# Moving a branch ahead of a shared block, building a routing table block by block, and turning outputs later, in a four-layer kernel

## The chip, the core and the metric

The kernel runs on one core of a Trainium2 chip. The core has engines with queues of their own: TensorE (PE, matrix products and turns), VectorE (DVE), ScalarE (ACT), GpSimd (POOL), and SyncE (SP), which here only issues DMAs; ACT and POOL issue some too. Each engine works through its instructions in the order in which the program has them, and semaphores tie the engines together. The time is that of the device for one execution, in microseconds (us), as the median of several runs. The kernel before takes 2748.42 us (three runs, 2748.25 to 2751.44).

## What is computed

Four layers work on 2048 tokens (8 sequences of 256) of 512 channels. Each adds an attention-like part and a feed-forward part, every one behind a layer norm and scaled by a gate:

```python
x = x + tanh(g_xattn[l]) * xattn_l(layernorm(x), ctx)
x = x + tanh(g_ffn[l])   * ffn_l(layernorm(x))
```

Three of these parts matter here. Layer 1's feed-forward part chooses 8 of 64 experts for each token and adds a shared expert:

```python
out = moe_out + silu(x @ sh_gate) * (x @ sh_up) @ sh_down
```

Layer 2's part is gelu(x @ p1 + b1) @ p2 + b2 with 2048 hidden units. Layer 3's attention is a recurrence over the 256 tokens of a sequence, channel by channel (WKV, with running sums aa and bb and a running maximum pp); its feed-forward part takes the best 2 of 8 experts and a shared MLP:

```python
scores = softmax(x @ gate_w.T); topk_w, topk_i = top_k(scores, 2)
eo = (silu(x @ w_gate[e]) * (x @ w_up[e])) @ w_down[e]      # of each expert e
y  = sum of topk_w * eo over the two choices + silu(x @ sw_gate) * (x @ sw_up) @ sw_down
```

## The kernel before

The tokens stand in 16 tiles of 128 (`P`), in 4 blocks of 512 (`BLK`, `NB` = 4, `TB` = 4 tiles). The 512 channels are 4 chunks of 128 (`KC`). The residual x of all tokens stays in SBUF. Three functions run one after the other: `front()` is layer 0, `middle()` layer 1, `back()` layers 2 and 3. A scheduler places each engine's instructions by the order in which the program makes them and by what they depend on; `behind(one, other)` and `held` add hints of order without a wait. Pools of a fixed number of buffers decide when a buffer can be used again: `t2` has 8 tiles of 128x512, `mm`, `tr` and `ac` are PSUM.

**The end of layer 1.** Every routed pair of tiles (`Pair`, 56 of them) loads an expert's weights, gathers its tokens, and runs gate and up products, a turn on PE (`turn`), and down products (`down`, L1286), whose result POOL adds to a table in memory, `acc`, by an indirect accumulating DMA. `shared1(blk)` is the shared expert of a block: three products (shg, shu, shr), then two steps of down products (shd). For the last block it is made as `end`, and `experts1` takes the first three of its steps as `between`, ahead of the last pair's turn; the rest comes after the last pair. Only then come a read of a flag and a branch (L1328 to L1332) to further pairs of tiles, which run only if more experts need a second tile than were planned for; with these inputs they don't.

```python
end = shared1(NB - 1, again)
experts1(pairs, (next(end) for _ in range(3)))
for _ in end:
    pass
some = nc.values_load(needing[0:1, 0:1], ...)
with tc.If(some > PAIRS1):
```

**The start of layer 2.** `back()` first fills layer 3's empty table (`table`, 39 tiles of 128 rows of a token's number and a weight) and the zero rows of `xnd` on POOL, and SP writes them out. `combine` (L1343) loads what the experts added (`more<-acc`) and adds it to x; the norm and the first attention products of layer 2, s, follow.

**Layer 2 beside layer 3's recurrence.** `ffn2(blk)` runs 4 quarters of hidden units, each 4 times h2p (4 products of 0.86 us, each two records in the trace) and 4 times o2f (also 4 products). Beside it the generator `tail(blk - 1)` is advanced: `step(2)` after each h2p, `step(1)` after each o2f. A tail is `xattn3` (the recurrence, one pass of DVE, POOL and ACT for each of 4 chunks, then the turned result y is added to x, L1520) and `route` (norm f3, the router's logits, the best two). `held` places a step's DVE operation behind the add of the product of the other block. When the last quarter's first o2f is done, `step(1000)` runs what is left. For the last block, tail(3) is advanced by `shared3()`, the shared MLP: for each block six steps (m = 5, 0 to 4; products sg and su) and two of down products (sd). `step(2)`, five times `step(5)` and twice `step(3)` belong to a block. In `xattn3` the last block yields five times more ahead of y (L1514 and the line after).

**The routing of layer 3.** After `SH0` = 15 steps of `shared3` and what is left of the tail, the whole table is built at once: how many tokens chose each expert (`cnt`), each choice's place (`pos`, `key`), rows and weights (`row_i`, `pay`), and 32 indirect writes from POOL (L1878), one for each tile and choice. SP reads the table back (`slots`), after `SH1` = 7 more steps DVE casts the token numbers (`who`, L1899), and `routed(n)` runs for 36 tiles: POOL gathers the expert's weights w (L1903) and the tokens xg (L1912), PE turns xg (tr_xg), and the products follow, with the remaining 9 steps of `shared3` between them. The results of `shared3` (`ys`) are added to the output by DMAs that POOL issues (L1804).

Of the kernel before, what the change touches and what calls it, by code (L numbers as in the profile page):

```python
# [20 lines left out]
P = 128  # L21
C = 512
# [17 lines left out]
SH0, SH1 = 15, 7  # L40
# [6 lines left out]
def flamingo_kernel(ctx: ExitStack, tc: tile.TileContext, a):  # L47
# [83 lines left out]
    def behind(one, other, reason):  # L131

        tc.add_manual_dep(
            one.ins,
            other.ins.name,
            mybir.DependencyInfo(mybir.DependencyClass.NoSync, mybir.DependencyReason.SCHED_ONLY),
            reason=reason,
        )
# [504 lines left out]
    def middle():  # L643
        with ExitStack() as st:
# [592 lines left out]
            class Pair:  # L1237


                def __init__(self, c, alike):  # L1240
                    self.c, self.alike = c, alike
                    self.w = []
                    self.more = t2.tile([P, C], F32, tag="t2", name=f"wd{c}")
                    for n in range(1 if alike else 2):
                        e = nc.values_load(
                            order[0:1, c + n : c + n + 1],
                            engines=[mybir.EngineType.SP],
                            min_val=0,
                            max_val=E1 - 1,
                            skip_runtime_bounds_check_because="each of the 64 ranks is one expert's",  # L1250
                        )
                        one = bass.ds(e, 1)
                        self.w.append(weight(a["w1"][one].rearrange("o p c -> (o p) c"), f"w1_{c + n}", ahead=c < 4))
                        nc.sync.dma_start(
                            self.more[rows_of[n]], a["wd1"][one].rearrange("o p c -> (o p) c")
                        )
                    self.w = (self.w * 2)[0:2]
                    self.buf = b8.tile([P, 2, C + I1 + 2 * P], F32, tag="b8", name=f"eb{c}")
                    self.tiles = []
                    self.tile()  # L1260
# [33 lines left out]
            def experts1(pairs, between=()):  # L1294

                rest = None
                pair = Pair(*pairs[0])
                for n in range(len(pairs)):
                    act = pair.first(0)
                    if pair.alike:  # L1300
                        behind(nc.scalar.copy(pair.more[rows_of[1]], pair.more[rows_of[0]]), act, "it comes late")
                    pair.tile()
                    if rest is not None:
                        rest.tiles[1].turn()
                        rest.down()
                    rest = pair
                    if n + 1 < len(pairs):
                        pair = Pair(*pairs[n + 1])
                    rest.first(1)
                    rest.tiles[0].turn()  # L1310
                for _ in between:
                    pass
                rest.tiles[1].turn()
                rest.down()
# [9 lines left out]
            end = shared1(NB - 1, again)  # L1324
            experts1(pairs, (next(end) for _ in range(3)))
            for _ in end:
                pass
# [3 lines left out]
            with tc.If(some > PAIRS1):  # L1331
                experts1([(PAIRS1 + E1 + 2 * n, False) for n in range((E1 - PAIRS1) // 2)])  # L1332
# [80 lines left out]
    def ffn2(blk, b8, wp, b1, gb2, step, last):  # L1413
        xT = turned2.pop(blk)

        for q in range(HID // BLK):
            h = b8.tile([P, KC, BLK], F32, tag="b8", name=f"h2_{q}_{blk}")
            p2 = []
            for j in range(KC):
# [10 lines left out]
                step(2, one)  # L1430
# [17 lines left out]
    def xattn3(blk, b8, lp, u, w, held):  # L1448
# [65 lines left out]
        if blk == NB - 1:  # L1514
            yield from (None,) * 5
# [13 lines left out]
    def back():  # L1529
        with ExitStack() as st:  # L1530
# [13 lines left out]

            xnd = dp.tile([NT + P, C], F32, tag="xnd3", name="xnd3")
            table = dp.tile([P * NS3, 2], F32, tag="table3", name="table3")
            rows_of_slot = table.rearrange("(p n) c -> p n c", p=P)
            empty = lp.tile([P, NS3, 2], F32, tag="empty3", name="empty3")
            nc.gpsimd.memset(empty, 0.0)
            nc.gpsimd.iota(  # L1550
                empty[:, :, 0], pattern=[[0, NS3]], base=NT, channel_multiplier=1, allow_small_or_imprecise_dtypes=True
            )
            nc.sync.dma_start(rows_of_slot, empty)
            zero = t2.tile([P, C], F32, tag="t2", name="zero3")
            nc.gpsimd.memset(zero, 0.0)
            nc.sync.dma_start(xnd[NT : NT + P, :], zero)
# [15 lines left out]
            )  # L1572
            part = lp.tile([P, 1], F32, tag="part3", name="part3")
# [4 lines left out]
            nc.sync.dma_start(gw, a["gwT3"].rearrange("p (k e) -> p k e", k=KC))  # L1578
# [4 lines left out]
            nc.vector.memset(run[:, 0, :], 0.0)  # L1583
            xT = []

            def route(blk):
# [18 lines left out]
                for i in range(TB):  # L1605
                    t = blk * TB + i
                    nc.vector.tensor_tensor(run[:, t + 1, :], run[:, t, :], sel[:, t, :], ALU.add)

# [51 lines left out]
            first_loads.append(loaded)  # L1660
            loaded = combine(range(TB, 2 * TB))
# [156 lines left out]
            wide = [P, TT, 8]  # L1818
            cnt = ac.tile([P, 8], F32, tag="ac", name="cnt3")
            nc.tensor.matmul(cnt, onesb, run[:, TT, :], start=True, stop=True)  # L1820
            pos = ac.tile(wide, F32, tag="ac", name="pos3")
            nc.tensor.matmul(pos, before, sel, start=True, stop=False)
            nc.tensor.matmul(pos, onesb, run[:, 0:TT, :], start=False, stop=True)

            def tiles_of(dst, src, plus):

                nc.vector.tensor_scalar(dst, src, 1.0 / P, plus / P - 0.498, ALU.mult, ALU.add)
                nc.vector.tensor_scalar(dst, dst, ROUND, None, ALU.add)
                nc.vector.tensor_scalar(dst, dst, -ROUND, None, ALU.add)

            tl = lp.tile([P, 8], F32, tag="tl3", name="tl3")
            tiles_of(tl, cnt, P - 1.0)
            ends = lp.tile([P, 8], F32, tag="ends3", name="ends3")
            nc.vector.tensor_tensor_scan(
                out=ends, data0=tl, data1=zero[:, 0:8], initial=0.0, op0=ALU.add, op1=ALU.add
# [6 lines left out]
            base = lp.tile([P, 8], F32, tag="base3", name="base3")  # L1842
            nc.vector.scalar_tensor_tensor(base, ends, 1.0, tl, ALU.add, ALU.subtract)
            fl = lp.tile(wide, F32, tag="fl3", name="fl3")
            tiles_of(fl, pos, 0.0)
            key = lp.tile(wide, F32, tag="key3", name="key3")
            nc.vector.scalar_tensor_tensor(
                key, pos, float(NS3), base.unsqueeze(1).to_broadcast(wide), ALU.mult, ALU.add
            )
            nc.vector.scalar_tensor_tensor(key, fl, 1.0 - NS3 * P, key, ALU.mult, ALU.add)  # L1850
            nc.vector.tensor_tensor(key, key, sel, ALU.mult)
            first = lp.tile([P, TT], F32, tag="first3", name="first3")
            other = lp.tile([P, TT], F32, tag="other3", name="other3")
            nc.vector.tensor_reduce(first, key, AX.X, ALU.max)
            nc.vector.tensor_reduce(other, key, AX.X, ALU.add)
            nc.vector.tensor_tensor(other, other, first, ALU.subtract)
            row_i = lp.tile([P, TT, 2], I32, tag="row3", name="row3")
            for j, r in enumerate((first, other)):
                nc.vector.tensor_tensor(fl, key, r.unsqueeze(2).to_broadcast(wide), ALU.is_equal)
                nc.vector.tensor_tensor(fl, fl, comb, ALU.mult)  # L1860
                nc.vector.tensor_reduce(pay[:, :, j, 1], fl, AX.X, ALU.add)
                nc.vector.tensor_scalar(row_i[:, :, j], r, -1.0, None, ALU.add)
# [11 lines left out]

            writes = []
            for t in range(TT):
                for j in range(2):
                    one = nc.gpsimd.indirect_dma_start(  # L1878
                        out=table[:, :],
                        out_offset=bass.IndirectOffsetOnAxis(ap=row_i[:, t, j : j + 1], axis=0),  # L1880
                        in_=pay[:, t, j, :],
                        in_offset=None,
                    )
                    tc.declare_no_dep(one.ins, group="table3", reason="choices have slots of their own")
                    tc.add_to_no_dep_group("table3", one.ins)
                    writes.append(one)
            slots = lp.tile([P, NS3, 2], F32, tag="slots3", name="slots3")
            load = nc.sync.dma_start(slots, rows_of_slot)
# [7 lines left out]
            for n in range(SH1):  # L1896
                next(more)
            who = lp.tile([P, NS3], I32, tag="who3", name="who3")
            behind(nc.vector.tensor_copy(who, slots[:, :, 0]), last_mul[0], "the table comes late")  # L1899

            def routed(n, one_more=False):
# [31 lines left out]
                tile3(f"r{n}", xgT, wgu, slots[:, n, 1:2], wd, add)  # L1933
# [105 lines left out]
```

## Time and profile before

One execution was profiled. It took 2773.92 us, its span is 2772.2.

| stage (us of the span) | PE busy | DVE busy | POOL busy | PE clock granted |
|---|---|---|---|---|
| 1520 to 1552, end of layer 1 | 12.93 of 32 | 14.32 | 5.62 | 0.72 |
| 1552 to 2166, layer 2 and tails | 589.91 of 614 | 360.53 | 141.60 | 0.98 |
| 2166 to 2200, start of shared3 | 29.89 of 34 | 26.63 | 4.93 | 0.95 |
| 2200 to 2280, last recurrence | 75.03 of 80 | 54.23 | 33.45 | 0.98 |
| 2280 to 2391, routing | 88.15 of 111 | 29.97 | 46.83 | 0.91 |
| 2391 to 2772, routed tiles | 366.24 of 381 | 68.58 | 127.56 | 0.98 |

A line of the waits names the engine and what it would have run, what released it, and the microseconds in total, how often, and the longest. A line of the timeline has start, duration, engine, line, operation, output and inputs, and in brackets how long the engine had been idle and who released it. L174 is a line of the kernel as printed above. A product of 512 columns shows as two records; the granted clock is 1 at full rate.

### The profile page before, as it was taken

The page shows a single profiled execution, that of the slowest core. Times are in us where ns is not written, and L with a number is a line of the kernel's source. Part 1 is how long each engine was busy: PE and PEld are TensorE (multiplying, and loading weights), DVE is VectorE, ACT ScalarE, POOL GpSimd, SP SyncE. Part 2 cuts the span into 40 slices and gives each one's busy share as a digit, 9 for nine tenths or more (in the row PEclk, how much of TensorE's full clock was granted, in tenths as well). Part 3 has the DMA queues.
Part 4 walks back from the last instruction along what each step waited for, and adds up shares of the span by engine and source line. Part 5 has one row for each costly group of instructions (what it writes and reads, how often), then busy time and mean ns, then how long its engine had stood idle before and what let it go on. Part 6 is the DMA issues. An engine that isn't in the chain of part 4 may idle for free. (4 is left out here: it accounts for less than half of the span.)

```text
span 2772.2 us, 29438 instructions
## 1 busy us (share of the span) xinstructions
PE 2580.3 (93%) x10245; PEld 1364.2 (49%) x10260; DVE 1277.0 (46%) x3495; ACT 665.8 (24%) x1500; POOL 889.9 (32%) x812
## 2 busy tenths in 40 slices
PE   7889998999999899999999799899999989799998
PEld 3454544456555445555555244344444434355554
DVE  7657665446644622222222732768566763111111
ACT  2534343211111113333332111222222221011111
POOL 1111111113434445565554110322323243433332
PEclk9999999999999899999999899999999999899999
DMA  5000000111100159999996812021121212688985
GB/s 209 9 20 20 20 35 5 40 47 43 62 24 24 57 173 241 241 242 249 240 250 126 281 40 99 29 89 50 61 91 68 95 15 71 208 276 268 300 268 120
DMA packets 96281, 332.86 MB, mean 120 GB/s; under 512 B 20863, under 2 KB 23167, under 8 KB 88192
## 3 DMA queue, kind: packets, MB, share of 16 engines
q0 software_dynamic: 45808, 156.38, 22.6%
q1 hardware_dynamic: 47440, 170.30, 17.7%
q10 hardware_dynamic: 2880, 4.23, 0.5%
q8 instruction: 85, 1.39, 0.2%
q14 instruction: 68, 0.56, 0.1%
HBM read 280.37 MB, written 64.82 MB: 125 GB/s over the span
## 5 line engine op out<-in xcount | busy, mean ns | idle before, releaser
L207 PE MATMUL gu<-w,eb 128*128 128x352 f32 x896 | 285.7, 462 | 0.0
L1286 POOL DMA_INDIRECT acc<-eb,who x112 | 177.4, 1584 | 184.2 <-DVE eb L102 164.4
L207 PE MATMUL h2p<-xnT_f,p 128*128 128x512 f32 x512 | 228.3, 602 | 2.4 <-ACT xnT_f L104 2.4
L207 PE MATMUL o2f<-p,h 128*128 128x512 f32 x512 | 226.4, 597 | 0.7 <-ACT h L1429 0.7
L207 PEld LDWEIGHTS gu<-w,eb 128*128 128x128 f32 x896 | 162.6, 192 | 73.0 <-issue 2.3
L947 POOL DMA_INDIRECT table<-pay,rowi x128 | 126.1, 985 | 148.7 <-issue 27.2
L536 ACT ACTIVATE pr<-pr,n 128x256 f32<-128x256 f32 x256 | 127.9, 501 | 150.0 <-DVE n L531 147.1
L207 PEld LDWEIGHTS h2p<-xnT_f,p 128*128 128x128 f32 x512 | 98.0, 193 | 122.5 <-issue 117.6
L207 PEld LDWEIGHTS o2f<-p,h 128*128 128x128 f32 x512 | 96.9, 191 | 119.4 <-issue 115.6
L1206 POOL DMA_INDIRECT xg<-xnd,who x112 | 117.6, 1050 | 61.4 <-PE ehp L1233 23.1
L218 DVE SCALAR_TENSOR_TENSOR x<-o2f,tg,x 128x512 f32<-128x512 f32 x64 | 47.8, 749 | 160.8 <-PE o2f L207 160.8
L1696 PE MATMUL g_r<-w,xgT 128*128 128x352 f32 x288 | 111.9, 470 | 0.7 <-ACT xgT L104 0.7
L1429 ACT ACTIVATE h<-h2p,b 128x512 f32<-128x512 f32 x64 | 43.0, 686 | 288.9 <-PE h2p L207 288.8
L1696 PE MATMUL u_r<-w,xgT 128*128 128x352 f32 x288 | 108.7, 459 | 0.0
L188 PE MATMUL tr_xg<-ident,xg 128*128 128x128 f32 x592 | 93.3, 281 | 13.7 <-DMA xg<-xnd,who 13.7
L1277 PE MATMUL ed<-w,eb 128*128 128x512 f32 x224 | 105.4, 593 | 0.0
L1719 PE MATMUL d_r<-w,hT_r 128*128 128x512 f32 (+1 forms) x216 | 104.2, 592 | 0.0
L188 PEld LDWEIGHTS tr_xg<-ident,xg 128*128 128x128 f32 x592 | 69.0, 142 | 70.7 <-issue 50.6
L102 DVE COPY eb<-ed 128x512 f32<-128x512 f32 x56 | 38.7, 692 | 137.8 <-PE ed L1277 137.8
L531 DVE CUSTOM_DVE_ANT_0 pr<-s,mask 128x256 f32<-128x256 f32 x256 | 96.8, 416 | 11.6 <-PE s L511 8.2
L1703 DVE SCALAR_TENSOR_TENSOR h_r<-a_r,slots,u_r 128x352 f32<-128x352 f32 x36 | 20.9, 581 | 175.9 <-PE u_r L1696 172.7
L1223 DVE SCALAR_TENSOR_TENSOR eb<-eb,share,gu 128x176 f32<-128x176 f32 x112 | 44.0, 393 | 122.2 <-ACT eb L1222 77.7
(530 smaller groups left out, 4717.6 us busy)
## 6 DMA issues: line engine op xcount, KB each, us to landing
w<-in_w SPq DMA_DIRECT2D x64, 960.0 KB
p<-in_p SPq DMA_DIRECT2D x64, 512.0 KB
xnd<-xn_f SPq DMA_DIRECT2D x32, 256.0 KB
acc<-xnd SPq DMA_DIRECT2D x32, 256.0 KB
more<-acc SPq DMA_DIRECT2D x32, 256.0 KB
wd<-in_wd SPq DMA_DIRECT2D x64, 96.0 KB
ctxTa<-in_ctxT SPq DMA_DIRECT2D x4, 1024.0 KB
x<-in_x SPq DMA_DIRECT2D x16, 256.0 KB
```

Of the source, the lines that this page charges most:

```text
L188: one = nc.tensor.transpose(ps[:, k, :], src[:, ts(k, P)], ident)
L207: one = nc.tensor.matmul(ps, lhsT[k], rhs[k], start=(k == 0), stop=(k == n - 1))
L218: return nc.vector.scalar_tensor_tensor(xt[i], ps, scale, xt[i], ALU.mult, ALU.add)
L531: one = nc.vector.tensor_tensor_reduce(pr[:, nt, :], ps[r][:, nt, :], mask[:, nt, :], -1.0, -LOW, ALU.add, ALU.min, n16[:, nt, h : h + 1],)
L536: nc.scalar.activation(pr[:, nt, :], pr[:, nt, :], AF.Exp, bias=n16[:, nt, h : h + 1], scale=-1.0, accum_out=s16[:, nt, h : h + 1],)
L947: one = nc.gpsimd.indirect_dma_start(out=table[:, :], out_offset=bass.IndirectOffsetOnAxis(ap=rows, axis=0), in_=choice, in_offset=None, b ...
L1206: nc.gpsimd.indirect_dma_start(out=xg, out_offset=None, in_=xnd[:, :], in_offset=bass.IndirectOffsetOnAxis(ap=who[:, c : c + 1], axis=0), ...
L1223: nc.vector.scalar_tensor_tensor(self.h, self.h, share[:, c : c + 1], gu[:, I1 : 2 * I1], ALU.mult, ALU.mult)
L1277: one = nc.tensor.matmul(ps[n], t.hT[rows, k, :], wd, start=(k == 0), stop=(k == 1))
L1286: nc.gpsimd.indirect_dma_start(out=acc[n][:, :], out_offset=bass.IndirectOffsetOnAxis(ap=who[:, t.c : t.c + 1], axis=0), in_=t.x, in_offse ...
L1696: nc.tensor.matmul(ps[:, 0:I3], xTt[:, k, :], wgu[k][:, g, :], start=(k == 0), stop=(k == KC - 1))
L1719: one = nc.tensor.matmul(ps, hT[:cn, n, :], wd[n][:cn], start=(n == 0), stop=(n == 2))
```

## The change

Five things change.

- Layer 1: `experts1` no longer takes steps of the last shared block. The branch follows it at once, and `shared1(NB - 1)` runs as a whole after the branch. The branch's own pairs take buffers of `wpool`.
- Layer 3's table gets a region of 2048 rows for each expert. It is emptied after the first `combine` and `context(0)`, no longer at the start of `back()`. The router's weights gw are loaded by ACT, no longer by SP.
- `route(blk)` now computes places, rows and weights for its own block and issues the block's 8 writes. With the regions, a choice's row needs only its expert and its rank there, not the counts of all blocks.
- After the last block, only counts, tile numbers and the first row of each of the tiles are computed. POOL reads the table by one indirect gather of 128 rows of 1 KB, PE turns the two halves (tokens, weights), DVE and ACT copy them out.
- Steps: 3 instead of 2 after each h2p from the third quarter on; the last block yields 10 times, not 5, before y; SH0, SH1 are 18, 4 instead of 15, 7.

```diff
-SH0, SH1 = 15, 7
+SH0, SH1 = 18, 4
...
-            def experts1(pairs, between=()):
+            def experts1(pairs):
...
                     rest.first(1)
                     rest.tiles[0].turn()
-                for _ in between:
-                    pass
                 rest.tiles[1].turn()
                 rest.down()
...
-            end = shared1(NB - 1, again)
-            experts1(pairs, (next(end) for _ in range(3)))
-            for _ in end:
-                pass
+            experts1(pairs)
             some = nc.values_load(
...
             with tc.If(some > PAIRS1):
-                experts1([(PAIRS1 + E1 + 2 * n, False) for n in range((E1 - PAIRS1) // 2)])
+                experts1([(PAIRS1 + E1 + 2 * n, False, (wpool, "w")) for n in range((E1 - PAIRS1) // 2)])
+            for _ in shared1(NB - 1, again):
+                pass
...
-                step(2, one)
+                step(2 if q < 2 else 3, one)
...
         if blk == NB - 1:
-            yield from (None,) * 5
+            yield from (None,) * 10
...
-            table = dp.tile([P * NS3, 2], F32, tag="table3", name="table3")
+            table = dp.tile([(E3 * TT + 1) * P, 2], F32, tag="table3", name="table3")
+            halves = table.rearrange("(h p) c -> h (p c)", p=P)
...
-            nc.sync.dma_start(gw, a["gwT3"].rearrange("p (k e) -> p k e", k=KC))
+            nc.scalar.dma_start(gw, a["gwT3"].rearrange("p (k e) -> p k e", k=KC))
...
+                pos = ac.tile(wide, F32, tag="ac", name=f"pos3_{blk}")
+                one, other = nc.tensor.matmul(pos, before, sel[:, tb, :], start=True, stop=False), latest[0]
+                behind(one, other, "the choices take their time")
+                nc.tensor.matmul(pos, onesb, run[:, tb, :], start=False, stop=True)
+                key = lp.tile(wide, F32, tag="key3", name=f"key3_{blk}")
+                nc.vector.tensor_tensor(key, pos, e2048.unsqueeze(1).to_broadcast(wide), ALU.add)
+                nc.vector.tensor_tensor(key, key, best, ALU.mult)
...
+                for t in range(blk * TB, blk * TB + TB):
+                    for j in range(2):
+                        one = nc.gpsimd.indirect_dma_start(
+                            out=table[:, :],
+                            out_offset=bass.IndirectOffsetOnAxis(ap=row_i[:, t, j : j + 1], axis=0),
+                            in_=pay[:, t, j, :],
+                            in_offset=None,
+                        )
...
             context(0, loaded)
             first_loads.append(loaded)
+            emptied()
...
-            load = nc.sync.dma_start(slots, rows_of_slot)
+            load = nc.gpsimd.indirect_dma_start(
+                out=slots.rearrange("h p c -> h (p c)"),
+                out_offset=None,
+                in_=halves,
+                in_offset=bass.IndirectOffsetOnAxis(ap=row_t[:, 0:1], axis=0),
+            )
...
+            who_ps = tr.tile([P, 2, P], F32, tag="tr", name="who3_ps")
+            other = latest[0]
+            for n in range(2):
+                one = nc.tensor.transpose(who_ps[:, n, :], slots[:, :, n], ident)
+                if n == 0:
+                    behind(one, other, "the table comes late")
             who = lp.tile([P, NS3], I32, tag="who3", name="who3")
-            behind(nc.vector.tensor_copy(who, slots[:, :, 0]), last_mul[0], "the table comes late")
+            behind(nc.vector.tensor_copy(who, who_ps[:, 0, 0:NS3]), last_mul[0], "the table comes late")
+            share = lp.tile([P, NS3], F32, tag="share3", name="share3")
+            nc.scalar.copy(share, who_ps[:, 1, 0:NS3])
```

## The prediction

> **What bounds it now.** The page's first part says TensorE: 2580.3 of 2772.2 us busy, 93%, and no other engine over 46%. The chain of waits ends in one output DMA and says nothing here, so I read next what PE waits for (us in total, times, longest), since only idle or half-clock PE time can be won. The largest wait of the run, and those between 2140 and 2460:
>
> ```profile
> PE s L207 <- DVE xn_a__0_12289 L174: 19.1, 1, 19.1
> ```
>
> ```profile
> PE y L1520 <- POOL xnT_a L1510: 8.8, 2, 6.5
> PE tr_xg L188 <- DMA xg<-xnd,who: 8.3, 1, 8.3
> PE sd L1792 <- issue: 6.9, 4, 2.5
> PE tr_f L188 <- DVE xn_f L174: 4.2, 2, 3.8
> ```
>
> The first is the seam between layers 1 and 2; the others surround layer 3's routing. Elsewhere on the changed paths PE waits little. So the sum has three places. All durations are of the profiled execution (2773.92 us, 1.7 around its span). It lies 25.5 us, 0.9%, above the median of 2748.42; I carry differences over unscaled, since 0.9% of 25 us is 0.2.
>
> **Seam of layers 1 and 2.** From the timeline (start, us, engine and operation, [idle before <- releaser]):
>
> ```profile
> 1528.18 1.55 POOL L1286 DMA_INDIRECT acc<-eb,who  x1 [0.30 <-issue]
> 1535.77 0.17 POOL L1549 MEMSET empty<- 128x78 f32 x1 [6.04 <-DMA acc<-eb,who]
> 1542.63 1.43 DVE L1343 TENSOR_TENSOR x<-x,more 128x512 f32<-128x512 f32 x2 [3.88 <-DMA more<-acc]
> 1550.34 2.05 PE L207 MATMUL s<-xn_a__0_12289,kxvs 128*128 128x512 f32 x2 [19.07 <-DVE xn_a__0_12289 L174]
> ```
>
> An accumulate lands 7.6 us after its issue; the reads of acc, the norm and PE follow in series. Now block 3's shared products lie before it, half inside the last pair, half after. Moved behind the branch, they run while the accumulates land. The last pair's turn then follows at once (DVE's h reaches PE at about 1512.7, 0.7 us idle), and its down products end at about 1516.1. The first accumulate must wait for the previous one on the same table (issued at 1510.25 in the timeline, + 7.6 = 1517.9), the second issues near 1519.7 and lands near 1527.3, not 1535.8. PE meanwhile has shg, shu, shr (four products of 0.86 each, 3 x 3.43) and shd (14 records of 0.43, 6.02), to 1533.4. SP's loads of acc start about 1528.2, after shr, land at 1532.5; DVE's first add stands behind the four shared adds, which end at 1534.9; from add to s takes 7.7 us (1542.63 to 1550.34). So s starts at 1542.6: **7.7 us won**, 9.2 still idle. ACT has 2 us to spare: shg's silu stands behind the small loads that ACT issues (gw is now one of them) and behind an Exp that waits for the decay's landing, ends near 1525.4, and PE needs its product at 1527.4. The emptying of the new table and its three SP DMAs leave the head of this chain; the POOL memsets (about 1 us) now stand ahead of later norms, under the adds. The branch cost DVE 0.27 us here; later code behind it is not shown, so 0.3 to 3. Bounds: 3 to 10 won.
>
> **Blocks 0 and 1: the earlier y.** With step(3) for q>=2, tail(0) and tail(1) reach their y products in the third quarter's o2f, after 8 of its 16, instead of 6 products into the fourth quarter: 14 x 0.86 = 12 us earlier in PE's order. The chain behind y must keep up. Its last pass in tail(1) before, and the one in tail(2), which already runs without waits on o2f:
>
> ```profile
> 2007.66 0.75 DVE L218 SCALAR_TENSOR_TENSOR x<-o2f,tg,x 128x512 f32<-128x512 f32 x1 [2.08 <-PE o2f L207]
> 2011.10 0.75 DVE L218 SCALAR_TENSOR_TENSOR x<-o2f,tg,x 128x512 f32<-128x512 f32 x1 [1.29 <-PE o2f L207]
> 2014.53 0.75 DVE L218 SCALAR_TENSOR_TENSOR x<-o2f,tg,x 128x512 f32<-128x512 f32 x1 [2.08 <-PE o2f L207]
> 2015.20 3.34 DVE L1508 RECIPROCAL den<-den 128x512 f32<-128x512 f32 x1
> 2019.94 0.66 PE L1520 MATMUL y<-ident,xnT_a 128*128 128x128 f32 x4 [0.30 <-POOL xnT_a L1510]
> ...
> 2140.30 3.34 DVE L1508 RECIPROCAL den<-den 128x512 f32<-128x512 f32 x1
> ...
> 2161.24 3.35 DVE L1508 RECIPROCAL den<-den 128x512 f32<-128x512 f32 x1 [1.38 <-POOL bb L1464]
> 2166.01 1.09 PE L1520 MATMUL y<-ident,xnT_a 128*128 128x128 f32 x8 [2.38 <-POOL xnT_a L1510]
> ```
>
> DVE's idle 2.08 and 1.29 are evacuations ahead of the chain in DVE's order. With them a pass takes 27.5 us from reciprocal to reciprocal (1987.73, the one before this, to 2015.20); without, 20.9 (2140.30 to 2161.24). The changed order has both bb scans ahead of aa, which saves the 1.38 and one scan more: 18.3. Reciprocal at 1987.7 + 18.3 + 3.34 + POOL's 1.3 puts xnT_a at 2010.8; PE arrives at 1986.9 + 24 x 0.86 = 2007.5. So PE waits about 3.5 us, 3.2 more than now, and the same in tail(0).
>
> Here a rule speaks against the change. The Trainium skill ("TensorE: Matmul & The Clock Gate", HAM oscillation) says that PE gaps above about 3.4 us put it at half clock, and its table gives about 3.4 us of work to recover: 1.7 lost. The rows agree at both sides. After 6.47 us the granted clock of 2286 to 2292 was 0.52, that of the next 8 us 1.00, and sg took 5.79 instead of 3.60. After 3.80 tr_f took 1.54 instead of 1.09; after 2.38 y ran at full rate, 1.09 for 8. A gap of 3.5 lies on the edge: by the rule 1.7 a block, by the 2.38 row nothing; I take 1.0. **8.4 us lost** in two blocks; bounds 1 (chain in time) and 20.
>
> Each block also gets its eight table writes on POOL, 8 x 1.28 = 10.2 us (0.97 and 0.30 between them). Behind them in POOL's order stands rstd_a. From pos to tr_a PE has 18 us (block 0) and 16.6 (block 1); the key operations take some 3 us, then the writes end at +13.3, before rstd_a's input at +15: covered. Cover gone, each us is one of PE. pos itself is two small matmuls and some 15 DVE operations of 0.15 to 0.3 in DVE's idle time.
>
> **Layer 3's routing.** Block 2's y now finds the chain ready to 1.4 us and tr_f lies inside the last o2f. Waits of 2.38 and 3.80 go. But what is late next is shgu, layer 3's shared weights, four loads of 704 KB into buffers that the last o2f frees: issued at 2171.4, and sg began at 2176.55, so the landing lay beside these waits. Now it is bare, some 4 us, and y waits 1.4: with half the cold products saved only **1.6 us won** (-2 to 5).
>
> For the last block, y stands one step (sg and su, 6.87 us) later: PE, which was there at 2279.9, comes at 2279.9 - 1.6 + 6.87 = 2285.2, and the chain, 1.6 earlier too, ends at 2284.8. With the hand-over, 6.47 becomes about 0.5 and y starts at 2285.7. Then the table:
>
> ```profile
> 2366.27 0.97 POOL L1878 DMA_INDIRECT table<-pay,row  x1 [0.30 <-issue]
> 2367.23 1.95 POOL L1804 DMA_DIRECT2D out_dram<-ys  x2
> ...
> 2378.15 0.95 POOL L1912 DMA_INDIRECT xg<-xnd,who  x1 [5.07 <-issue]
> ```
>
> 32 writes ran from 2326.4 to 2367.2. They held the output DMAs behind them in POOL's order, these held t2 buffers, and so DVE and sd: the 6.9 of "issue". Then who and xg, which landed 12.4 us after its issue behind w of 2.2 MB each. Changed, only eight writes remain, some 2327.5 to 2337.8; w_0, the gather, w_1 to w_3 issue by 2345. PE's work from y to tr_xg, at full rate, is 82.3 us of the timeline's products (SH0 + SH1 is still 22, so none is added), less the one now ahead of y: from 2285.7, 6.87 taken off what follows, it arrives at about 2361. slots (128 KB, behind w_0) is there at 2348; PE's two transposes stand behind four products and come at 2352, then the copy of who, and xg issues at 2354. PE's small turns cost it 0.3. The Trainium skill ("DMA: Bandwidth & Descriptors", Anatomy of one DMA) prices 256 KB at 2.0 us + bytes/436 GB/s, 2.6: xg at 2357, no wait. The row speaks of a queue: w_1 issued at 2369.5 and xg landed 21 us later with it. From 2341.5 that is 2363, and four w are now in flight at once, where w_0 was long there before: 2365. I take the row. Of 22.9 us idle (y 6.5, two small waits 1.2, sd 6.9, xg 8.3) and 5.4 at half clock (sg 2.2, the last ten sd records 7.20 instead of 4.3, and 0.3) some 4.5 remain: **23.8 won**. Bounds 14 (xg at 2375) and 28. The routed loop after it keeps its order and its PE bound.
>
> **Sum:** -7.7 + 8.4 - 1.6 - 23.8 = -24.7; 2748.4 becomes **2724**.
>
> **Rivals.**
> 1. The routed table is not early: the gather waits for the write landings and xg for 8.9 MB of w. Xg at 2375 leaves 10 us more idle: 2734. For it: the 12.4 us above. Against: 30 us fewer writes ahead.
> 2. The y stalls stay small, the seam loses its cold restart too: 8 + 2 less, 2714. For: the 20.9 row is itself a contended pass. Against: 3.80 already went cold.
> 3. Slower: the chain behind y is bound by DVE, POOL and ACT, not by o2f. Four passes in a row take 27.5 us. If that stays, y waits 12.4 us in blocks 0 and 1, 12.1 more than now, and in block 2 (chain ready at 2140.3 + 27.5 + 4.6 = 2172.4, PE there at 2155.8) 16.6, 14.2 more; each with 2 us at half clock: 44 lost. Against it 31.5 won at seam and table: +13, 2761. It decides from passes of some 26.5 us, where three times 8 us more eat the 24.7. For it speaks that no other pass is shown at 20.9; against it, the idle rows above.
> 4. The change doesn't do what it says at the branch: code behind it comes late, or the accumulates still end the chain; the seam gains nothing: 2732.
>
> **Chances.** Forecast 0.48, with 2717 to 2731 its own; rival 1 0.17, rival 2 0.17, rival 3 0.10, rival 4 0.08. The range for 8 in 10, 2710 to 2740, takes in rivals 1, 2 and 4. A measurement of this kernel tells 0.2%, 5.5 us. Faster 0.87: all but rival 3 and a tail of rivals 1 and 4; within 0.05; slower 0.08, most of rival 3.
>
> **What would show it.** s after the seam at some 9 us of wait, with shd just before. y in blocks 0 and 1 at some 3.5 us each. No wait on sd "issue"; tr_xg at 3 to 8. sg at stage start behind shgu. Wrong if y waits 10 us, or rstd_a is released by table writes, or tr_xg still waits 8 or more.

## The result and the profile after

| | median us | runs | lowest to highest |
|---|---|---|---|
| before | 2748.49 | 8 | 2744.56 to 2752.11 |
| after | 2739.19 | 8 | 2735.15 to 2745.19 |

The ratio is 0.9966 (95% interval 0.9953 to 0.9979): 9.3 us faster (5.8 to 12.9), where 24.7 were forecast. The direction is right, and of the sum a good third is there.

The profiled execution of after took 2745.19 us, 6 above its median; its page begins so:

```profile
span 2743.4 us, 29494 instructions
...
PE 2570.1 (94%) x10253; PEld 1360.1 (50%) x10268; DVE 1283.8 (47%) x3535; ACT 671.7 (24%) x1505; POOL 894.0 (33%) x814
```

One thing spoils a look at absolute times: the first 1000 us of the program, which no kernel here changes, took 1011.2 us in the profile of before and 985.8 in that of after, and the kernel before had medians of 2748, 2767 and 2776 in the sets of runs that follow. So I compare times within one set, and profiles from layer 1's first product `gu` on. From it the two kernels end after 1761.0 and 1757.6 us. A single profile still tells no more than a few us: before and experiment 2, the same up to there, reach layer 2's first h2p 1.6 us apart.

What TensorE waits for, in the stretch from layer 2's start to the first routed tiles (1560 to 2450; us in total, times, longest), and, from the whole run, the seam:

```profile
PE y L1517 <- POOL xnT_a L1507: 12.0, 3, 4.5
...
PE tr_xg L188 <- DMA xg<-xnd,who: 4.3, 1, 4.3
PE tr_a L188 <- DVE xn_a L174: 4.2, 2, 3.9
PE sd L1839 <- DVE ys L1848: 4.2, 1, 4.2
```

```profile
PE s L207 <- DVE xn_a__0_12285 L174: 8.8, 1, 8.8
```

The big waits went as forecast: s from 19.1 to 8.8, tr_xg from 8.3 to 4.3, no y of 6.5 for the last block, no sd on "issue". What is new is y: 12.0 in three waits, where the blocks 0 to 2 had 0.3, 0.3 and 2.4. But the waits don't add up to the time, so each place has to be looked at.

**The seam.** TensorE's timeline, after:

```profile
1489.79 1.13 PE L1277 MATMUL ed<-wd,eb 48*128 48x512 f32 x4
1494.34 5.37 PE L207 MATMUL shg<-xnT_f,shgu 128*128 128x512 f32 x8 [3.42 <-DVE run L1590]
1499.55 3.60 PE L207 MATMUL shu<-xnT_f,shgu 128*128 128x512 f32 x8
1502.98 3.60 PE L207 MATMUL shr<-xnT_f,shgu 128*112 128x512 f32 x8
1506.41 5.91 PE L1117 MATMUL shd<-shd,shT 128*128 128x512 f32 x16
1521.18 2.08 PE L207 MATMUL s<-xn_a__0_12285,kxvs 128*128 128x512 f32 x2 [8.85 <-DVE xn_a__0_12285 L174]
```

Between the last expert product and shg nothing runs for 3.42 us, and shg then takes 5.37 instead of the 3.60 of its equal shu: half clock (the granted clock was 0.67 in shg's stretch, 1.00 in shu's). The releaser named, `run`, is DVE's first instruction behind the branch, and it was itself released by TensorE's sequencer (PEq):

```profile
1494.21 0.06 DVE L1590 MEMSET run<- 128x4 uint32 x1 [2.56 <-PEq L1326]
```

So the engines meet behind the branch, and TensorE came last. The records of the branch's line on the engines' sequencers show why (engine, operation, times; ns; start), first after, then before:

```profile
L1326 PEldq COMPARE_BRANCH  x1: 3892/3892/3892, 1490.1 to 1490.1; - x1
L1326 ACTq COMPARE_BRANCH  x1: 45/45/45, 1491.5 to 1491.5; - x1
L1326 DVEq COMPARE_BRANCH  x1: 76/76/76, 1491.6 to 1491.6; - x1
```

```profile
L1331 PEldq COMPARE_BRANCH  x1: 3727/3727/3727, 1525.9 to 1525.9; - x1
```

On TensorE the branch takes 3.9 us (and reading the flag ahead of it 1.1), on the other engines 0.05 to 0.08. Before, TensorE's sequencer took it 5.4 us ahead of the last shared product's end, beside products that were already queued. After, only 0.8 us of products are left when it takes it.

**y in blocks 0 and 1.** TensorE's timeline, after:

```profile
1824.63 1.12 PE L1517 MATMUL y<-ident,xnT_a 128*128 128x128 f32 x4 [4.47 <-POOL xnT_a L1507]
1825.54 5.35 PE L207 MATMUL o2f<-p,h 128*128 128x512 f32 x8
1830.73 0.60 PE L1517 MATMUL y<-ident,xnT_a 128*128 128x128 f32 x4
1831.16 3.60 PE L207 MATMUL o2f<-p,h 128*128 128x512 f32 x8
...
1994.95 1.12 PE L1517 MATMUL y<-ident,xnT_a 128*128 128x128 f32 x4 [4.47 <-POOL xnT_a L1507]
1995.86 5.53 PE L207 MATMUL o2f<-p,h 128*128 128x512 f32 x8
```

Both blocks wait 4.47 us, and the first y and eight records of o2f after it cost 2.3 and 2.5 us more than the next ones (granted clock 0.63 and 0.62).

**The routing.** POOL's timeline, after:

```profile
2332.57 0.97 POOL L1643 DMA_INDIRECT table<-pay,row  x1 [0.31 <-DMA table<-pay,row]
2333.85 1.02 POOL L1932 DMA_INDIRECT w<-in_w,wrow  x1 [0.30 <-DMA table<-pay,row]
2338.23 0.97 POOL L1904 DMA_INDIRECT slots<-table,row_t  x1 [3.37 <-DMA table<-pay,row]
...
2349.89 0.96 POOL L1941 DMA_INDIRECT xg<-xnd,who  x1 [6.92 <-DVE who L1926]
```

Eight writes instead of 32, the gather behind the last one's landing, and xg at 2349.9, which TensorE has at 2361.8: 11.9 us behind the w of 2.2 MB, as in the row that the forecast took (12.4). From the last block's first y to the first routed product (g_r) the new routing takes 80.9 to 81.5 us in the six profiles that have it with ten yields, the old one 107.2 to 108.7 in six. Of the difference 6.87 us are the step that now stands ahead of y.

### The profile page after: what moved, and what is told of

It is laid out like the page before. It is cut to its first block, busy times and chain, and to the rows that moved or that the text cites. A ratio compares the mean times of both kernels' runs of the same rounds, so it can differ in the third digit from the quotient of the medians.

```text
span 2743.4 us, 29494 instructions
## 1 busy us (share of the span) xinstructions
PE 2570.1 (94%) x10253; PEld 1360.1 (50%) x10268; DVE 1283.8 (47%) x3535; ACT 671.7 (24%) x1505; POOL 894.0 (33%) x814
## 3 DMA queue, kind: packets, MB, share of 16 engines
q1 hardware_dynamic: 47154, 170.34, 18.3%
## 5 line engine op out<-in xcount | busy, mean ns | idle before, releaser
L207 PE MATMUL h2p<-xnT_f,p 128*128 128x512 f32 x512 | 235.6, 617 | 2.6 <-ACT xnT_f L104 2.6
L1743 PE MATMUL u_r<-w,xgT 128*128 128x352 f32 x288 | 108.7, 459 | 0.0
L1750 DVE SCALAR_TENSOR_TENSOR h_r<-a_r,share,u_r 128x352 f32<-128x352 f32 x36 | 20.9, 580 | 176.1 <-PE u_r L1743 172.9
```

The source lines that it names most:

```text
L207: one = nc.tensor.matmul(ps, lhsT[k], rhs[k], start=(k == 0), stop=(k == n - 1))
L1743: nc.tensor.matmul(ps[:, 0:I3], xTt[:, k, :], wgu[k][:, g, :], start=(k == 0), stop=(k == KC - 1))
```

## The experiments

Three questions: what ate the seam's gain, what y's early place costs, and whether the rest is as large as the sum had it. Ratios are to the kernel before in the same set of runs.

**1. After, without layer 1's branch.** The path for more experts than planned is left out.

```diff
             experts1(pairs)
-            some = nc.values_load(...)
-            with tc.If(some > PAIRS1):
-                experts1([(PAIRS1 + E1 + 2 * n, False, (wpool, "w")) ...])
             for _ in shared1(NB - 1, again):
```

> The changed kernel without the branch of layer 1 (the read of its flag and the pairs of tiles behind it, which these inputs don't run; the path for overflowing experts is left out). Theory BRANCH: in the changed kernel PE's own compare-and-branch (3.9 us) and flag read (1.1) stand bare ahead of shg, and 3.4 us of idle time put shg at half clock (5.37 instead of 3.60). Without it shg follows the last down products at once: PE's wait before shg under 0.6, and 4 to 6 us less than the changed kernel (ratio to before near 0.995, from 0.9966). Rival ACCUMULATES: the seam is set by the landing of the last accumulates and the loads behind it; then shg comes early but s starts no earlier, its wait grows from 8.8 to about 13, and the time stays at 0.9966.

2736.57 us, ratio 0.9952 (0.9939 to 0.9966): 2.6 us under after by the medians, less than expected, and the two intervals overlap. The profile is plainer: no wait ahead of shg, and s 7.3 us earlier (528.0 us after gu, not 535.3), with its own wait unchanged:

```profile
1511.90 2.08 PE L207 MATMUL s<-xn_a__0_11733,kxvs 128*128 128x512 f32 x2 [8.86 <-DVE xn_a__0_11733 L174]
```

So s follows the shared products; the accumulates don't set it.

**2. Before, with step(3) alone.**

```diff
-                step(2, one)
+                step(2 if q < 2 else 3, one)
```

> The kernel before with one edit: step(3) instead of step(2) after h2p from the third quarter on. Theory Y-EARLY: y of tail(0) and tail(1) comes ahead of the end of its chain, PE waits 4.5 us there twice and runs at half clock after it; 10 to 14 us slower than before (ratio 1.004 to 1.005). Rival WRITES: what blocks 0 and 1 lose in the changed kernel comes from the eight table writes on POOL; then this kernel, which has none there, is within 0.1% of before. Rival CLOCK: the loss is half-clock stretches that come and go by themselves; then also within 0.1%.

2768.28 us, ratio 1.0072 (1.0058 to 1.0086): 19.9 slower, more than expected. TensorE's waits from 1560 to 2480:

```profile
PE tr_xg L188 <- DMA xg<-xnd,who: 20.7, 1, 20.7
PE y L1520 <- POOL xnT_a L1510: 18.4, 4, 6.5
```

No block has its table writes here, and y waits all the same: the writes are not its cause. From the first h2p of block 1 to that of block 2 it takes 170.3 us, before 163.1: 7.2 for one early y. The 20.7 at tr_xg is not the step's doing: experiment 4, which has the old steps, shows 20.1 there and no wait on sd "issue", and from the last y to the first routed product the two take 108.5 and 107.8 us, before 107.2. Two blocks at 7.2 make 14.4; the rest of the 19.9 is not explained, so it is not the price of y alone. Experiment 3 gives that.

**3. After, with y two steps later in blocks 0 to 2.**

```diff
-        if blk == NB - 1:
-            yield from (None,) * 10
+        yield from (None,) * (10 if blk == NB - 1 else 2)
```

> The changed kernel with two more yields ahead of y for the blocks other than the last, so that y of tail(0) and tail(1) stands 8 products (6.9 us) later on PE, while the steps stay quick. Theory Y-EARLY: the waits of 4.5 before y vanish in both blocks, with the half-clock products after them, and nothing else moves: 10 to 14 us less than the changed kernel (ratio to before 0.9915 to 0.993). Rival WRITES: the table writes are then nearer to rstd_a, and tr_a waits instead: no gain, 0.9966. Rival CLOCK: no gain either, and no wait before tr_a.

2726.57 us, ratio 0.9919 (0.9905 to 0.9932): 12.9 us less than after by the ratios (0.9966 - 0.9919 = 0.0047 of 2748), which by their intervals is an estimate of 8 to 18. The waits of blocks 0 and 1 are gone:

```profile
PE y L1516 <- POOL xnT_a L1507: 3.0, 1, 3.0
```

The rows above say the same: 4.47 - 0.3 in each of two blocks, and 2.3 and 2.5 at half clock, are 13.1. So this is the price of y's early place, and the chain needs only two steps. The two profiles lie further apart, 20.6 us from `gu` on. Some 3.6 of the rest is mostly half clock at the end of block 2, from the first y there to the first sg (27.8 us after, 24.2 in experiment 3); it is in the profiles of after and of experiment 1, and what sets it off is not known.

**4. Before, with the seam's part alone.**

```diff
-            end = shared1(NB - 1, again)
-            experts1(pairs, (next(end) for _ in range(3)))
-            for _ in end:
-                pass
+            experts1(pairs)
             some = nc.values_load(...)
             with tc.If(some > PAIRS1):
-                experts1([(PAIRS1 + E1 + 2 * n, False) ...])
+                experts1([(PAIRS1 + E1 + 2 * n, False, (wpool, "w")) ...])
+            for _ in shared1(NB - 1, again):
+                pass
```

> The kernel before with the first part of the change alone: the branch ahead of the whole last shared block. Theory BRANCH: 2 to 6 us faster than before (0.998 to 0.9993), with PE idle about 3.4 us before shg and some 9 to 12 before s, since the old emptying of the table still stands at the head of back() here. The prediction's own figure for this part was 7.7. Rival ACCUMULATES: the landing sets s and the seam gains the full 7 to 8 us (0.9972).

2748.62 us, ratio 0.9997 (0.9989 to 1.0005): nothing, where a gain was expected.

**5 and 6. Y later, with another seam.** In 5 shg, shu and shr stand ahead of the branch, behind the last pair, in a buffer of their own; in 6 the seam is that of before. All else is experiment 3.

```diff
             experts1(pairs)
+            end = shared1(NB - 1, again)
+            for _ in range(3):
+                next(end)
             some = nc.values_load(...)
...
-            for _ in shared1(NB - 1, again):
+            for _ in end:
                 pass
```

> The kernel with y later (changed kernel, two more yields), and shg, shu and shr of the last shared block made ahead of the branch, after the last pair, with buffers of b8 so that the branch's pairs don't wait for them; only shd stays behind the branch. Theory BRANCH: PE's sequencer stands at the branch while the matmuls already issued still run, as in the kernel before (its compare-and-branch of 3.7 us began 5.4 us ahead of the last shd's end), so the 3.9 us lie beside products: PE's wait at the branch under 1 us, 3 to 6 us less than y later alone (ratio to before 0.9897 to 0.9908). Rival FETCH: PE can't fetch behind a branch before it has drained; then some 3 us of wait stand ahead of shd and the time stays at 0.9919.

> The kernel with y later, its seam as in the kernel before (three shared products inside the last pair, the rest ahead of the branch). Theory BRANCH and the run of the seam alone: the branch's move is worth nothing where its 5 us stand bare; the time stays within 3 us of y later (0.991 to 0.993). Rival: the seam alone gained nothing only because the old emptying of the table stood at the head of back(); with it moved the new seam is worth 4 to 8, and this kernel is that much slower (0.9935 to 0.995).

Number 5: 2744.24 us beside 2776.27 of before in its set, ratio 0.9895 (0.9880 to 0.9910), the best of all kernels here, though its interval touches that of experiment 3. The hiding worked only in part: shd waits 2.05 us, not under 1, and then takes 9.23 us instead of the 5.91 of after. TensorE's own branch was covered. It ended at 1518.8, 2.7 us ahead of the end of shr; but the engines meet behind it, and here DVE came last, whose flag read and branch stand behind its product with shr:

```profile
L1334 PEldq COMPARE_BRANCH  x1: 4478/4478/4478, 1514.3 to 1514.3; - x1
L1334 DVEq COMPARE_BRANCH  x1: 76/76/76, 1522.8 to 1522.8; - x1
```

Number 6, in the same set: 2752.16, ratio 0.9917 (0.9904 to 0.9931), which is that of experiment 3 (0.9919). Once more the seam as changed is worth nothing. And number 6 holds all else of the change without the early y: 0.0083 of 2748, 22.8 us won.

**7 and 8. Other steps.** In 7, after with `step(2, one)` throughout; in 8, experiment 3 with 5 yields for the last block, not 10.

> The changed kernel with step(2) in all quarters, so that y stands where it stood before and the tails run as slowly as before. Theory Y-EARLY with a second term: the waits before y go (12 us), but pos of block 1 then comes only 8 us of PE's work ahead of tr_a, while the eight writes (10.2 us) and rstd_a stand between on POOL; tr_a of tail(2) waits 5 to 8 us and goes cold. Net 2 to 8 us less than the changed kernel (0.9937 to 0.996). Rival: the writes are hidden at either place; then all 12 are won, 0.992.

> The kernel with y later, but with 5 instead of 10 yields ahead of y of the last block. Theory: y of the last block then stands one step (6.87 us) earlier and waits 5 to 7 us for its chain with half a clock after it; the rest of the routing follows earlier by the step, but ends at the same xg. 2 to 8 us slower than y later (0.9926 to 0.995). Rival: the wait only replaces the one of 4.6 at tr_xg, and the time stays at 0.9919.

Number 7 missed: 2770.92 us, ratio 0.9983 (0.9976 to 0.9990), no better than after (0.9966, to 0.9979) and rather slower. y waits 3.0 in all, but now the block's table writes come later and stand in POOL's order ahead of the next norm, which TensorE needs. POOL's timeline, then TensorE's:

```profile
2058.87 1.04 POOL L1643 DMA_INDIRECT table<-pay,row  x1 [8.29 <-DVE hit L1635]
...
2067.80 0.96 POOL L1643 DMA_INDIRECT table<-pay,row  x1 [0.30 <-issue]
2068.78 1.05 POOL L166 TENSOR_TENSOR rstd_a<-ve_a,mhalf 128x4 f32<-128x4 f32 x1
```

```profile
2070.56 1.94 PE L188 MATMUL tr_a<-ident,xn_a 128*128 128x128 f32 x8 [7.27 <-DVE xn_a L174]
```

Here is the loss that the forecast named for the case that the writes' cover goes. The step of 3 is needed for the writes; only y should not come with it, and experiment 3 parts the two. Number 8: 2761.3, ratio 0.9953 (0.9939 to 0.9967), 0.0034 or 9.3 us worse than experiment 3 by the ratios, more than expected; TensorE's waits say why:

```profile
PE y L1516 <- POOL xnT_a L1507: 9.4, 2, 6.4
```

The last block's y is back at 6.4, as before the change, with half clock after it. This profile also has a wait of 3.3 us on a load of layer 2 (kxvs), 1.0 in experiment 3, which the edit does not touch; how much it adds to the 9.3 is open.

**9, 10 and 11. The seam by itself, with a control.** All three are the kernel before with edits at the seam only: in 9 that of experiment 4 without flag read and branch, in 10 only flag read and branch are left out, in 11 experiment 4 with shg, shu and shr ahead of the branch as in 5. In 9 and 10 the path for more experts than planned is left out.

> The kernel before with the seam's part of the change alone, and without layer 1's flag read and branch (the path for more experts than planned is left out). BRANCH (the bare branch ate the seam's gain: 3.4 us idle plus 1.8 at half clock): the predicted gain comes back, 5 to 9 us less than before, s about 11 us earlier against the first gate-up product (528 instead of 539), and the first h2p of layer 2 at 596 to 599 instead of 604. ABSORBED (what follows s until the first h2p is paced by something that the seam does not move, so an earlier s is lost again): s about 11 earlier too, but h2p not below 601 and the time at most 3 us less.

> Control: the kernel before with only the flag read and the branch left out, seam as it was (the path for more experts than planned is left out). BRANCH: TensorE's sequencer is done with the branch before the shared down products end, so nothing is gained, within 3 us of before, and s still waits 17 to 19 us. ABSORBED: the same, within 3. If the time falls by more than 4, the branch also costs something where it stood, and the price of moving it is smaller than said.

> The kernel before with the seam's part of the change alone, but with shg, shu and shr ahead of the branch (in a buffer of their own), and shd behind it. BRANCH: most of TensorE's branch lies beside shu and shr, some 2 us idle and 3 at half clock stay, so 2 to 6 us less than before. ABSORBED: at most 1.5 less.

Experiment 4 stands beside them, from another set; us after gu in the profiles, with the first h2p of block 1 in brackets:

| seam | branch | s | first h2p (of block 1) | ratio to before |
|---|---|---|---|---|
| before | as before | 539.1 | 604.0 (756.1) | 1 |
| before (10) | none | 533.8 | 598.8 (751.7) | 0.9988 (0.9979 to 0.9996) |
| changed (4) | ahead of all shared products | 535.3 | 604.8 (757.7) | 0.9997 (0.9989 to 1.0005) |
| changed (11) | behind shr | 531.3 | 596.7 (750.6) | 0.9978 (0.9970 to 0.9985) |
| changed (9) | none | 528.0 | 594.9 (747.0) | 0.9970 (0.9958 to 0.9981) |

The other profiles repeat these rows up to block 1. Its first h2p comes at 755.2 and 756.8 with the old seam (2 and 6), at 754.8 to 756.1 with the changed one (after, 3, 7, 8), at 748.3 with the changed one and no branch (1), and at 749.8 with the branch behind shr (5). So the groups stand apart by more than their spread, and old and changed seam with their branch do not.

Without the branch the changed seam gives 8.3 us (0.0030 of their before, 2766.95), about the 7.7 of the forecast, though 3.3 of them come from the branch's going and not from the move: what follows s does not absorb the gain. With the branch it gives none. The control moved a little more than expected, 3.3 us, and its s waits 14.9, not 19.1. There it is not TensorE that pays: the branch also keeps code from being placed ahead of it. In the kernel before, SP's first load behind it starts at 1531.43, as TensorE's sequencer comes through (1531.4). Without the branch POOL's emptying of layer 3's table and SP's writes of it are done before the last accumulates, and SP reads acc 6.3 us after the last of these is issued (1517.97 to 1524.23), not 10.2 (1528.18 to 1538.35). So between two seams without a branch the move is worth 5.0 us (8.3 - 3.3, some 4 either way), and with it 0.8, which can't be told from nothing: the branch costs the changed seam 7.5 us, and the old one 3.3 (1.1 to 5.8). Behind shr most of the branch is hidden, and 6.1 us are won (4.2 to 8.3); the 2.06 us that shd waits there are DVE's, as in experiment 5.

## Why the prediction was wrong

**The seam: "7.7 us won". This step failed.** "The last pair's turn then follows at once", and the products and loads after it, came much as worked out (its terms add up to 1532.4 for the end of shd, not 1533.4), and s waits 8.85 where 9.2 was said. The term that was mis-sized is "The branch cost DVE 0.27 us here; later code behind it is not shown, so 0.3 to 3". I took DVE's branch for TensorE's, whose 3.7 us stood in the trace of before, under its sequencer, hidden only by queued products. Bare, it leaves TensorE idle for 3.42 us and costs 1.8 at half clock. Those 5.2 don't make the whole 7.3 of experiment 1: without a branch two records of shg also fill TensorE's two waits in the last pair's turn (0.38 and 0.47), and 1.0 lies ahead of the last pair. From s to the first h2p experiment 4 took 69.5 us and after 66.4, before 64.9; but without a branch it is 66.9 and 67.2 (9 and 1), so this stretch is not the branch's, and what lengthens it stays open. Rival 4 was the true one here, in the words "code behind it comes late"; I gave it 0.08.

**Blocks 0 and 1: "8.4 us lost". The mechanism was right, the size was not:** 12.9 by experiments, 13.1 by the rows. The wait was 4.47, not 3.5 (the forecast's own terms give 2010.6 for xnT_a, so 3.1), because a pass took 19.6 us, not 18.3: 3.1 and these 1.3 are 4.4. DVE's timeline of after, from one reciprocal to the next, and POOL's beside it:

```profile
1796.84 0.68 DVE L1502 TENSOR_TENSOR den<-ex,bb 128x512 f32<-128x512 f32 x1
...
1800.27 3.34 DVE L1505 RECIPROCAL den<-den 128x512 f32<-128x512 f32 x1
...
1812.25 2.30 DVE L1490 TENSOR_TENSOR_SCAN bb<-ex 128x256 f32<-128x256 f32 x2 [3.31 <-ACT ex L1479]
1814.47 1.24 DVE L1485 TENSOR_TENSOR_SCAN aa<-ex,ev 128x256 f32<-128x256 f32 x2
...
1816.36 1.75 DVE L1502 TENSOR_TENSOR den<-ex,bb 128x512 f32<-128x512 f32 x1
...
1819.88 3.35 DVE L1505 RECIPROCAL den<-den 128x512 f32<-128x512 f32 x1 [1.16 <-POOL bb L1461]
```

```profile
1812.30 1.71 POOL L1482 TENSOR_TENSOR ev<-ex,ctxTc 128x512 f32<-128x512 f32 x1 [3.14 <-ACT ex L1479]
1815.86 1.70 POOL L1498 TENSOR_TENSOR ev<-ex,ctxTc 128x512 f32<-128x512 f32 x1 [1.85 <-DVE aa L1485]
...
1818.19 1.65 POOL L1503 TENSOR_TENSOR den<-den,ex 128x512 f32<-128x512 f32 x1 [0.59 <-DVE den L1502]
```

The order that I praised, both bb scans ahead of aa, puts them beside POOL's ev. den takes 1.75 us beside an ev and 0.68 without one a pass earlier; the two bb scans take 2.30, and the two of aa just after them, without an ev, 1.24. The pass of 20.9, from which I worked, had one such meeting of its own, as rival 2 said: before, num took 1.69 beside an ev.

```profile
2155.39 1.69 DVE L1502 TENSOR_TENSOR num<-ex,aa 128x512 f32<-128x512 f32 x1
```

```profile
2155.04 1.50 POOL L1501 TENSOR_TENSOR ev<-ex,ctxTc 128x512 f32<-128x512 f32 x1 [1.45 <-DVE aa L1488]
```

So den's meeting only takes num's place. What is new is the meeting of the scans, 1.0 us, and some 0.4 in POOL's last den (1.65, and 1.26 a pass earlier). The Trainium skill states the cause ("SBUF — State Buffer", Who interferes with whom): a DVE instruction with two SBUF inputs contends with a POOL one that reads SBUF. Both inputs of a bb scan are parts of ex. The rows agree: den ends 0.55 us after the ev that began ahead of it. And half clock cost 2.3 and 2.5, not 1.0: the rule of 1.7 that I weighed against it was the nearer one.

**Table, block 2 and last block: "1.6" and "23.8 won". Right in sum:** 25.4 forecast, 22.8 (19.0 to 26.4) by experiment 6. Block 2 fell short: y waits 3.02, not 1.4. What TensorE waits for next is the norm of block 3 (TensorE's timeline, after):

```profile
2149.16 1.29 PE L1517 MATMUL y<-ident,xnT_a 128*128 128x128 f32 x8 [3.02 <-POOL xnT_a L1507]
...
2175.68 1.51 PE L188 MATMUL tr_a<-ident,xn_a 128*128 128x128 f32 x6 [3.87 <-DVE xn_a L174]
2176.98 1.92 PE L207 MATMUL sg<-xnT_f,shgu 128*128 128x512 f32 x2
```

But shgu, which I named, is as late. Its four loads and their times to landing:

```profile
L1727 SPq DMA_DIRECT2D shgu<-in_shgu x4: 333/420/709, 2171.8 to 2173.2; - x4
DMA to landing us min/median/max: 4.2/6.1/8.0
```

The first landed at 2176.0, 4.2 us after the last o2f and 1.0 ahead of the first sg. So the "some 4 us" are there, and two things end them together; an earlier norm alone could have brought sg forward by 1.0 at most. The routing is as worked out: last y without a wait, tr_xg 4.3 where 4.5 was said, sd's waits on "issue" gone. (The 4.2 of sd on DVE's ys, in block 0 of the shared MLP, stands in both kernels.) By the profiles the last block won more than was said, some 26 us: 107.2 against 81.0 from its first y on, less the step of 6.87, plus y's wait of 6.5. Ahead of it some was lost, where 1.6 were to be won: from block 2's first h2p to the last y experiments 3, 5 and 6 take 357.9, 362.5 and 362.4 us, and before's 356.0, less y's wait and with the step more, make 356.4. What lost it is not shown. That the table writes of blocks 0 and 1 are covered held, by little: POOL is idle for 1.2 and 2.9 us between the last write and rstd_a, and experiment 7 takes the cover away.

**The sum:** 0 + 12.9 - 22.8 = -9.9, beside the 9.3 measured. That it closes proves little, since 12.9 and 22.8 are differences to experiments 3 and 6, which have nearly the same ratio; the 13.1 by the rows and experiment 4 stand on their own. Of the 15.4 us missed, 7.7 are the seam, where the branch ate the gain, 4.5 y, and about 2.6 the rest. The 2739.2 measured lie just inside the range of 2710 to 2740 and outside the forecast's own. Rival 1 fell (tr_xg waited as forecast), rival 2 (y stalls small) and rival 3 (passes of 27.5) too.

## What to carry to other kernels

A branch can cost one engine far more than the others (here TensorE 3.5 to 4.5 us, DVE 0.08), and the engines meet behind it, so the last one holds the rest. Read the sequencers' own records, cover the dear branch with queued work, and look at which engine then comes last: with TensorE's covered in experiments 5 and 11 it was DVE, and 2 us stayed. When steps of a side chain are speeded up, look at which step the main engine itself waits for; here the writes had to come earlier and y had not, and two empty steps ahead of y turned 9 us won into 22. A pass's length from one profile holds only for its order: a DVE instruction that took 0.68 us took 1.75 beside one of POOL.

## What was not expected of the hardware

- TensorE's branch took 3.5 to 4.5 us at layer 1's end (3.55 in experiment 4, 4.48 in experiment 5), the other engines' 0.05 to 0.08; at a second branch, at the end of the kernel, TensorE's took 0.37. What makes the difference was not tried.
- The length of a gap does not say whether half clock follows. TensorE waited 2.05 us ahead of shd in experiment 5 and 2.06 in experiment 11, and the same 16 records took 9.23 and 5.99 us, at a granted clock of 0.50 from 1526 to 1530 in 5 and 1.00 throughout in 11 (the idle before, then who released it, in brackets):

```profile
1523.59 9.23 PE L1122 MATMUL shd<-shd,sh 128*128 128x512 f32 x16 [2.05 <-DVEq L1334]
```

```profile
1525.32 5.99 PE L1122 MATMUL shd<-shd,sh 128*128 128x512 f32 x16 [2.06 <-DVEq L1336]
```

The 3.4 us that the Trainium skill names for such a gap ("TensorE: Matmul & The Clock Gate", HAM oscillation), which the forecast used as an edge, is none here.

- Clock was also lost with no gap at all. At the end of block 2, in the profile of after, TensorE shows no idle time from 2164 to 2171.8, and the granted clock was 0.69; the last four records of o2f took 3.76 us there, and 1.96 in experiment 3.
